# A two-layer graph network on one core: row-end products merged, identity products dropped, evictions moved

## The chip, the cores and the metric

The kernel runs on one core of a Trainium2 chip. The metric is the device time of one execution in microseconds (us). A core has five engines with queues of their own: PE (TensorE, matrix products), DVE (VectorE), ACT (ScalarE), POOL (GpSimd) and SP (SyncE, which here only issues DMAs). They meet through semaphores. Matrix products write to PSUM, eight banks of 512 f32 for each of 128 partitions; everything else lies in SBUF.

## The reference

`x` is 4096 nodes by 64 features, `adj` a 4096 by 4096 matrix of weights, under 1% of them not zero.

```python
h = relu(layernorm(x))
for k in range(2):                                  # layer 0, two hops
    h = tanh(concatenate([adj @ h, h], axis=1) @ W[k])
x = x + h
h = relu(layernorm(x))
support = h @ weight                                # layer 1
mask = adj != 0
rank = cumsum(mask, axis=1); deg = rank[:, -1:]
k = minimum(deg, 100); pos = rank - (deg - k)
w = mask * where(pos > 0, 0.5 ** (k - pos), 0.0)
out = x + w @ support + bias
```

So the dense matrix is used three times: twice with its values, and once as powers of two that depend on how many entries of the row come after.

## The kernel before, in words

Nodes are cut into 32 blocks of 128 (`NB`), four chunks of 8 blocks (`CB`, `NCH`). `adjA[I, n]` is the tile of row chunk I and block n, 128 by 1024 f32 (512 KB); a row chunk has 1024 output nodes, held in two halves of 512 columns (`C`, index c). PSUM holds accumulators `acc`/`accl` of three banks in a pool with two buffers (`pacc`), and two single banks, `one` and `two`.

**Sweep 1** (L370) takes the row chunks 0 to 3, each with 16 pairs of blocks, from the highest block to 0. For each pair: the DMA (1 MB, up to five pairs ahead, L396), the count of non-zero entries (`count_pair`, marks on DVE or ahead on ACT, kept as bytes in `codes`), and hop-0 products. Blocks whose hop-0 result isn't known yet multiply h alone into bank `acc[:, 2]` (`agg_pair`, L254, two 64-row products over 512 columns). Blocks of an earlier chunk (`fused`, L438) multiply `[h, x1]` (128 rows) into banks 0 and 1: hop 0 in the lower half of the partitions, hop 1's share in the upper.

When a row chunk ends, `finish_row` (L306) is queued; one step of it runs after each further pair. It copies S (bank 2) and F (banks 0, 1) out of PSUM, makes po = W0 products of S, F and of the node's own features in `pre1`, x1T = tanh(po); transposes x1T to nodes by a product with `ident` (`nodes`, L208); makes the hop-1 share po1 (features by nodes: `wz[:, 1, 1, 0]` with F, `wz[:, c, 1, 1]` with x1T) and keeps it in `pre1`; then `set_after` (L293) twice, with `tri` and with `neg`, from the totals of both halves and of the later half. Its output `after` is subtracted from the codes by `settle`. For the last row, `finish_last` (L473) does the same inside sweep 2; for row 0 the products of held blocks (`G`) are added.

**Sweep 2** (L771) computes hop 1 for the blocks not fused (72 blocks of 512 KB, ring of 6 then 4 slots) and, as soon as a chunk of x2 is ready, layer 1. `finish_x2` (L511) is a generator: identity products L518 bring the share in `pre1` into bank `py` as nodes, a second set L531 adds the rest, ACT takes tanh, DVE adds the residual `xres`, then a layer norm whose result is split in three bf16 parts: hi, mid (in `hx`) and lo. **Layer 1** goes in 64 units (J, g, n): chunk J of x2, row chunk g, two blocks. `convert` turns codes into powers of two, on DVE or ACT, into any free place (`spaces`). `layer1(n)` issues n units together: first all products of hi and mid (L692, `accl` banks 0 and 1, c = 0, 1), then all products of lo (L704, bank 2, c in the halves of the partitions). When the four units of a (J, g) are done and the sum isn't `kept` for the next J, its three banks are evicted into `part(g)`: a first one is copied by ACT and DVE (L725), later ones added by DVE (L729, L734). `finish_out` (L746) multiplies by `weight`, adds `pre1` and stores.

The order of the work is written by hand (`manual_schedule`): within sweep 1 by the pair loop, within sweep 2 by a planner that keeps a clock for each engine (`use`) and a list of due times (`chain`, `ready`, `due`), and emits conversions up to 2.5 to 10 us ahead of PE's clock (`lead`). Each engine runs what was emitted in that order; the waits between engines follow from the tiles.

Of the kernel before, what the change touches and what calls it, by code (L numbers as in the profile page):

```python
# [8 lines left out]
F32 = mybir.dt.float32  # L9
# [27 lines left out]
def gnn_kernel(  # L37
# [20 lines left out]

    nc = tc.nc

    N, D = x.shape
# [46 lines left out]
    xv = x.rearrange("(p b) d -> p b d", b=NB)  # L108
# [14 lines left out]
    def load_x(engine, b0, b1):  # L123
        engine.dma_start(pre1[:, b0:b1, :], xv[:, b0:b1, :])
# [7 lines left out]

    def load_weights():
        for h in range(2):
            rows = slice(h * D, (h + 1) * D)
            nc.sync.dma_start(wz[rows, h], Wd)
            nc.sync.dma_start(wa[rows], weight)
            nc.gpsimd.tensor_copy(wh[rows, h], wa[rows])

# [10 lines left out]
    ident = cpool.tile([P, P], F32, name="ident")  # L150
# [4 lines left out]
    neg = cpool.tile([P, P], BF16, name="neg")  # L155
    nc.vector.tensor_scalar(neg, diff, 0.0, -1.0, op0=ALU.is_equal, op1=ALU.mult)

    off = cpool.tile([P, 2], F32, name="off")
    for h in range(2):
        nc.vector.tensor_scalar(  # L160
            off[:, h : h + 1], diff[:, P - 1 : P], float(2 * FULL), float((1 - h) * FULL),
            op0=ALU.mult, op1=ALU.add,
        )
# [43 lines left out]

    def nodes(src):  # L208

        pt = one(name="pt")  # L210
        for t in range(TC):
            nc.tensor.matmul(  # L212
                pt[:, t * P : (t + 1) * P], by_t(src)[:, t // 2, t % 2, :], ident,
                start=True, stop=True, skip_group_check=True,
            )
        return pt.rearrange("p (t c e) -> p t c e", t=TC, c=NC)
# [67 lines left out]
    def totals(I):  # L284

        both = tmp([P, CW], U8, name="both")
        nc.vector.tensor_tensor(both.bitcast(U16), cnts[I % 2][0], cnts[I % 2][1], op=ALU.add)  # L287
        tot = [tmp([P, CW], BF16, name="tot") for _ in range(2)]
        nc.scalar.copy(tot[0], both)  # L289
        nc.scalar.copy(tot[1], cnts[I % 2][1].bitcast(U8))  # L290
        return tot

    def set_after(I, v, tot, banks):  # L293

        for c, pb in enumerate(banks):
            nc.tensor.matmul(  # L296
                pb, tri if v else neg, tot[1 - v][:, c * C : (c + 1) * C],
                start=v == 1, stop=True, skip_group_check=True,
            )
        for c, pb in enumerate(banks):  # L300
            nc.vector.tensor_scalar(  # L301
                after[:, v, I * CW + c * C : I * CW + (c + 1) * C], pb,
                off[:, v : v + 1], float(K), op0=ALU.add, op1=ALU.min,
            )

    def finish_row(I, acc, held):  # L306
        S = tmp(name="S")
        nc.scalar.copy(S, acc[:, NC, :])
        if I:
            F = [tmp(name="F") for _ in range(NC)]  # L310
            for c in range(NC):
                nc.scalar.copy(F[c], acc[:, c, :])
        tot = totals(I)
        yield
        po = one(name="po")
        terms = [(lambda c: wz[:, c, 0, 0], lambda c: S)]
        if I:
            terms.append((lambda c: wz[:, 0, 0, 0], lambda c: F[c]))
        x1T = x1_of(po, I, terms)
        po1 = two(name="po1")  # L320
        if I:
            for c in range(NC):
                nc.tensor.matmul(
                    po1[c * D : (c + 1) * D, :], wz[:, 1, 1, 0], F[c], start=True, stop=False
                )
        yield
        pt = nodes(x1T)
        for c in range(NC):
            nc.tensor.matmul(  # L329
                po1[c * D : (c + 1) * D, :], wz[:, c, 1, 1], x1T, start=I == 0, stop=I > 0  # L330
            )
        nc.scalar.copy(as_nodes(hx[:, chunk(I), D:]), pt)
        yield
        if I == 0:

            own = [v for k in sorted(held) for v in held[k]]
            for n, (b, a) in enumerate(own):
                agg_pair(acc[:, 0, :], hx[:, b, D:], a, n == 0, n == len(own) - 1)
            held.clear()
            G = tmp(name="G")  # L340
            nc.scalar.copy(G, acc[:, 0, :])
            yield
            for c in range(NC):
                nc.tensor.matmul(
                    po1[c * D : (c + 1) * D, :], wz[:, c, 1, 0], G, start=False, stop=True
                )
        nc.scalar.copy(flat(pre1[:, chunk(I), :]), po1)
        yield
        banks = [one(name="pb"), two(name="pb")]
        for v in (1, 0):  # L350
            set_after(I, v, tot, banks)
            yield
        all_settle(I)
# [16 lines left out]
    def sweep1():  # L370
        b0 = NB - 2
        load_x(nc.sync, b0, NB)
        load_x(nc.sync, NB - CB, b0)
# [26 lines left out]
        for k, (I, b) in enumerate(pairs):  # L400
# [3 lines left out]
            if k == 0:  # L404
                load(1, 0)
                load_x(nc.sync, NB - 2 * CB, NB - CB)
                load(2, 0)
                load_x(nc.sync, 0, NB - 2 * CB)
# [54 lines left out]
        return acc, totals(I)  # L463
# [9 lines left out]
    def finish_last(acc, tot):  # L473

        I = NCH - 1
        S = tmp(name="S")
# [4 lines left out]
        use("ACT", 1.7, 0.2)  # L481
# [7 lines left out]
        pt = nodes(x1T)  # L489
        nc.scalar.copy(as_nodes(hx[:, chunk(I), D:]), pt)  # L490
        use("ACT", 0.6, use("PE", 1.3) + 0.2)
        po1 = two(name="po1")
        for c in range(NC):
            nc.tensor.matmul(
                po1[c * D : (c + 1) * D, :], wz[:, 1, 1, 0], F[c], start=True, stop=False
            )
        for c in range(NC):
            nc.tensor.matmul(
                po1[c * D : (c + 1) * D, :], wz[:, c, 1, 1], x1T, start=False, stop=True
            )  # L500
        nc.scalar.copy(flat(pre1[:, chunk(I), :]), po1)
        use("ACT", 0.6, use("PE", 1.9) + 0.2)
        yield
        banks = [one(name="pb"), two(name="pb")]
        for v in (1, 0):
            set_after(I, v, tot, banks)
            use("DVE", 1.4, use("PE", 0.5) + 0.2)
            yield
        all_settle(I)

    def finish_x2(I, acc):  # L511

        h = chunk(I)

        pt = one(name="py")
        v = by_t(flat(pre1[:, h, :]))
        for t in range(TC):
            nc.tensor.matmul(  # L518
                pt[:, t * P : (t + 1) * P], v[:, t // 2, t % 2, :], ident,
                start=t == 0, stop=False, skip_group_check=True,  # L520
            )
# [3 lines left out]
        nc.sync.dma_start(xres, xv[:, h, :])  # L525
        t0 = use("ACT", 0.6, clock["PE"] + 0.2)
        use("PE", 1.25)
        yield t0 + 0.1
        v = by_t(S)
        for t in range(TC):  # L530
            nc.tensor.matmul(  # L531
                pt[:, t * P : (t + 1) * P].rearrange("p (c e) -> p c e", c=NC),
                v[:, t // 2, t % 2, :], wz[:, :, 1, 0, :],
                start=False, stop=True, skip_group_check=True,
            )
        y = tmp(name="y")
        nc.scalar.activation(y, pt, AF.Tanh)
        yield use("ACT", 0.65, use("PE", 1.25) + 0.2) - 0.5
        nc.vector.tensor_tensor(
            as_nodes(pre1[:, h, :]), as_nodes(xres), y.rearrange("p (t c e) -> p t c e", t=TC, c=NC),  # L540
            op=ALU.add,
        )
        t = use("DVE", 0.7, clock["ACT"] + 0.1)
# [132 lines left out]
    def layer1(n):  # L676
# [20 lines left out]
        use("PE", 0.2)  # L697
        for i, acc in zip(todo, accs):
# [10 lines left out]
        for i, acc in zip(todo, accs):  # L709
# [12 lines left out]
            if g not in parted:  # L722
                parted.add(g)
                for q, p in enumerate(part(g)):
                    (nc.vector.tensor_copy if q == 1 else nc.scalar.copy)(p, acc[:, q, :])  # L725
                    use("DVE" if q == 1 else "ACT", 0.65, t)
            elif J:
                for q, p in enumerate(part(g)):
                    nc.vector.tensor_tensor(p, acc[:, q, :], p, op=ALU.add)  # L729
                    use("DVE", 0.65, t)  # L730
            else:
                ys = part(g)
                for q, p in enumerate(ys):
                    nc.vector.tensor_tensor(p, acc[:, q, :], p, op=ALU.add)  # L734
                t = use("DVE", 1.9, t)
# [7 lines left out]

    outs = []

    def finish_out(g, ys):  # L746
        last = g == order[0][-1]
        pt = (one if g % 2 else two)(name="pto")
# [3 lines left out]
        for ks in [range(K4)] if not last else [range(K4 // 2), range(K4 // 2, K4)]:  # L752
            for k in ks:
                cols = slice(k * P, (k + 1) * P)
                for c in range(NC):
                    nc.tensor.matmul(  # L756
                        pt[:, k * P + c * D : k * P + (c + 1) * D], ys[c][:, cols], wa,
                        start=k == c == 0, stop=not last, skip_group_check=True,
# [12 lines left out]
    def sweep2(acc, tot):  # L771
# [7 lines left out]
        space(quad(mbuf.rearrange("p a r i -> p (a r i)").bitcast(I16)))  # L779
# [5 lines left out]
        last = finish_last(acc, tot)  # L785
# [92 lines left out]
    sweep2(*sweep1())  # L878
# [26 lines left out]
```

## Time and profile before

| what | us |
|---|---|
| median of 3 runs (lowest, highest) | 392.31 (390.9, 392.37) |
| profiled execution | 390.78 |
| its span | 389.0 |
| sweep 1 up to the last pair | 0 to 205.5 |
| layer 1 from its first product | 241.9 |
| last output stored | 387.95 |

In the profile, one f32 product is recorded as two matmuls, so `x8` under L254 is two blocks. Two 64-row products on different halves of the array run side by side: eight such records take 1.72 us, eight of 128 rows (L438) 3.48. Rates of the DMA queues from the page, in 40 slices of 9.7 us:

```profile
GB/s 229 415 411 406 365 408 407 409 408 409 410 345 270 313 327 235 205 291 305 293 350 317 250 417 401 182 283 305 304 265 224 313 312 258 2 2 2 0 56 54
```

The transfers are at their full rate, some 410 GB/s, up to about 110 us and again around 223 to 240.

### The profile page before, as it was taken

The numbers are of one execution on the slowest core, as the hardware profiler recorded it, in microseconds if no ns is written. First come the engines' busy times: TensorE is split into PE (matmuls) and PEld (weight loads), VectorE is DVE, ScalarE is ACT, GpSimd is POOL, SyncE is SP. The second block draws the span as 40 slices with busy tenths as digits, with TensorE's granted clock in tenths as the row PEclk, the third lists the DMA queues.
The fourth block names the chain that finished last, engine by engine and source line by source line (L and its number), as shares of the span: only waits on it lengthen the run. The fifth ranks groups of instructions, "written<-read, shape, count | busy, mean of one in ns | idle before, by whom it ended". The sixth has DMA issues, their size and how long they took to land.

```text
span 389.0 us, 4496 instructions
## 1 busy us (share of the span) xinstructions
PE 365.5 (94%) x1654; PEld 144.5 (37%) x1668; DVE 301.4 (77%) x565; ACT 166.2 (43%) x164; POOL 22.7 (6%) x21
## 2 busy tenths in 40 slices
PE   3698789999999999999999988999999999999995
PEld 0142223234333443444443323333343333434554
DVE  5979989499989999699889697777846844389943
ACT  2179980754363433410004111744246945388200
POOL 2202100000000000000000030300003000030000
PEclk9699999999999999999999999999999999999999
DMA  7999999999997896578999799588876887000011
GB/s 229 415 411 406 365 408 407 409 408 409 410 345 270 313 327 235 205 291 305 293 350 317 250 417 401 182 283 305 304 265 224 313 312 258 2 2 2 0 56 54
DMA packets 30150, 108.50 MB, mean 279 GB/s; under 512 B 2736, under 2 KB 3376, under 8 KB 30128
## 3 DMA queue, kind: packets, MB, share of 16 engines
q1 hardware_dynamic: 30128, 108.21, 75.0%
q8 instruction: 13, 0.21, 0.2%
q14 instruction: 9, 0.07, 0.1%
HBM read 107.15 MB, written 1.05 MB: 278 GB/s over the span
## 4 chain that ended last, share of the span: by engine, by line
PE 79%; DMA 13%; SPq 3%; ACT 2%; issue 1%; DVE 0%; ACTq 0%
PE acc L254 25%; PE acc L438 21%; PE accl L692 15%; PE accl L704 8%; DMA codes<-in_adjA_dram 8%; DMA ring<-in_adjA_dram 5%; SPq L396 3%; PE po L196 2%; PE pto L756 2%; PE pt L212 1%; ACT codes L227 1%; PE pb L296 1%; PE py L518 1%; ACT codes L228 1%; PE po L329 1%
## 5 line engine op out<-in xcount | busy, mean ns | idle before, releaser
L254 PE MATMUL acc<-ring,hx 128*64 128x512 f32 x384 | 95.6, 623 | 12.2 <-DVE hx L186 6.4
L438 PE MATMUL acc<-ring,hx 128*128 128x512 f32 x152 | 66.2, 593 | 0.0
L254 PE MATMUL acc<-codes,hx 128*64 128x512 f32 x256 | 59.3, 598 | 5.5 <-DMA codes<-in_adjA_dram 5.5
L254 PEld LDWEIGHTS acc<-ring,hx 128*64 128x64 f32 x384 | 25.6, 140 | 66.3 <-issue 31.6
L438 PEld LDWEIGHTS acc<-ring,hx 128*128 128x128 f32 x152 | 28.8, 190 | 36.0 <-issue 35.7
L248 DVE TENSOR_SCALAR lo<-codes 128x512 uint16<-128x512 uint16 x128 | 37.6, 294 | 4.4
L247 DVE TENSOR_TENSOR codes<-mbuf,lo 128x512 uint16<-128x512 uint16 x90 | 38.3, 425 | 3.1
L692 PEld LDWEIGHTS <-hx 128*128 128x128 bf16 x256 | 23.2, 98 | 39.7 <-issue 12.6
L366 DVE TENSOR_TENSOR codes<-codes,after 128x2048 uint16<-128x2048 uint16 x32 | 37.6, 1217 | 0.0
L183 POOL TENSOR_TENSOR s<-s,half 128x8 f32<-128x8 f32 (+2 forms) x9 | 16.7, 1852 | 323.1 <-DVE s L182 323.1
L236 DVE TENSOR_SCALAR mbuf<-ring 128x2048 uint8<-128x2048 f32 x27 | 32.9, 1220 | 2.0 <-DMA ring<-in_adjA_dram 2.0
L228 ACT ACTIVATE codes<-codes 128x1024 uint8<-128x1024 int8 x32 | 33.8, 1057 | 1.0
L254 PEld LDWEIGHTS acc<-codes,hx 128*64 128x64 f32 x256 | 17.7, 138 | 43.3 <-issue 30.5
L227 ACT ACTIVATE codes<-codes 128x1024 int8<-128x1024 f32 x24 | 25.1, 1047 | 16.1 <-DMA codes<-in_adjA_dram 16.1
L642 ACT ACTIVATE codes<-codes,zero 128x2048 int16<-128x2048 uint8 x14 | 27.2, 1992 | 9.7 <-PE accl L704 9.7
L692 PE MATMUL accl<-codes,hx 128*128 128x512 bf16 x118 | 29.2, 380 | 0.2
L642 ACT ACTIVATE ring<-codes,zero 128x2048 int16<-128x2048 uint8 x11 | 21.7, 1995 | 11.0 <-PE accl L704 11.0
L236 DVE TENSOR_SCALAR mbuf<-codes 128x2048 uint8<-128x2048 f32 x21 | 25.6, 1219 | 0.0
L301 DVE TENSOR_SCALAR after<-pb,off 128x512 uint8<-128x512 f32 x16 | 11.4, 745 | 13.3 <-PE pb L296 13.3
L289 ACT CAST tot<-both 128x1024 bf16<-128x1024 uint8 x4 | 4.2, 1057 | 37.7 <-DVE both L287 37.7
L692 PE MATMUL accl<-ring,hx 128*128 128x512 bf16 x74 | 18.8, 380 | 0.6 <-issue 0.2
L704 PEld LDWEIGHTS <-lo 128*64 128x64 bf16 x256 | 12.2, 109 | 19.0 <-issue 10.6
(109 smaller groups left out, 354.8 us busy)
## 6 DMA issues: line engine op xcount, KB each, us to landing
ring<-in_adjA_dram SPq DMA_DIRECT2D x74, 512.0 KB, 5.0
codes<-in_adjA_dram SPq DMA_DIRECT2D x33, 1024.0 KB, 12.5
ring<-in_adjA_dram SPq DMA_DIRECT2D x30, 1024.0 KB, 5.6
xres<-in_x_dram SPq DMA_DIRECT2D x4, 256.0 KB, 5.9
out_dram<-o SPq DMA_DIRECT2D x3, 256.0 KB, 2.5
pre<-in_x_dram SPq DMA_DIRECT2D x1, 512.0 KB, 9.8
pre<-in_x_dram SPq DMA_DIRECT2D x1, 256.0 KB, 6.8
out_dram<-o SPq DMA_DIRECT2D x2, 128.0 KB, 1.9
```

The source lines that it names most:

```text
L183: nc.gpsimd.tensor_tensor(s2, s2, half[:, :nb], op=ALU.pow)
L227: nc.scalar.activation(sign, a[:, r], AF.Sign)
L228: nc.scalar.activation(m, sign, AF.Square, scale=float((FLAG - 1 + 0.25) ** 0.5))
L236: nc.vector.tensor_scalar(m, a, 0.0, float(FLAG - 1), op0=ALU.not_equal, op1=ALU.mult)
L247: nc.vector.tensor_tensor(q, marks[r].bitcast(U16), cnt, op=ALU.add)
L248: nc.vector.tensor_scalar(cnt, q, 0x7F7F, None, op0=ALU.bitwise_and)
L254: nc.tensor.matmul(acc[c * D : (c + 1) * D, :], src, a[:, c * C : (c + 1) * C], start=first, stop=last,)
L366: nc.vector.tensor_tensor(q, q, a[:, None, :].to_broadcast([P, 4, CW // 2]), op=ALU.subtract)
L438: nc.tensor.matmul(acc[:, c, :], hx[:, g, :], a[:, r, c * C : (c + 1) * C], start=g == CB * I - 1, stop=g == 0,)
L642: nc.scalar.activation(w.rearrange("p r k x y -> p r k (x y)"), src.rearrange("p r (y k) -> p r k y", k=2), AF.Relu, scale=float(FLAG), bi ...
L692: nc.tensor.matmul(like(accs[-1][:, c, :], w), hm[:, CB * J + 2 * k + r, : 2 * D], w[:, r, c], start=first and r == 0, stop=last and r == 1,)
L704: nc.tensor.matmul(like(acc[c * D : (c + 1) * D, 2, :], w), lo[:, CB * J + 2 * k + r, :], w[:, r, c], start=first and r == 0, stop=last an ...
```

## The change

Six edits come together.

1. At the ends of rows 1 and 2 the sums are stacked: `T[c]` holds bank c's lower half over the c-th half of bank 2, so that one product with `w0` (hop 0's W twice) replaces two. The upper halves of banks 0 and 1 go to `Fx`.
2. `x1_and_share` multiplies x1T once with `both_w` = [ident, W1], 256 columns, into banks `one` and `two`: x1 as nodes and the share of hop 1, both by nodes. `take` copies each out in two parts. The share is kept by nodes in `pre1`, so `finish_x2` has no identity products; it adds the share on DVE before the tanh, and yields before its products, not after the first of them.
3. `set_after` uses `tri` only; the early half follows from the late one and the later half's count by three byte operations on DVE.
4. `x` is handed over as four chunks, [4, 128, 8, 64]; each is one DMA, and chunk 3 is loaded whole before the first tile.
5. In `layer1`, banks 0 and 1 of a finished sum are evicted between the hi and the lo products of the batch (`evict`), bank 2 after the lo products. First evictions are all on ACT.
6. The two halves of the last output use different banks.

```diff
-    def load_x(engine, b0, b1):
-        engine.dma_start(pre1[:, b0:b1, :], xv[:, b0:b1, :])
+    def load_x(q):
+        nc.sync.dma_start(pre1[:, chunk(q), :], x[q])
...
-    def set_after(I, v, tot, banks):
-
+    def set_after(I, tot, banks):
+
+        cols = slice(I * CW, (I + 1) * CW)
         for c, pb in enumerate(banks):
-            nc.tensor.matmul(
-                pb, tri if v else neg, tot[1 - v][:, c * C : (c + 1) * C],
-                start=v == 1, stop=True, skip_group_check=True,
-            )
+            nc.tensor.matmul(pb, tri, tot[:, c * C : (c + 1) * C], start=True, stop=True)
...
+        early = after[:, 0, cols]
+        nc.vector.tensor_scalar(
+            early.bitcast(U16), cnts[I % 2][1], -1.0, float(FULL * 257), op0=ALU.mult, op1=ALU.add
+        )
+        nc.vector.tensor_tensor(
+            early.bitcast(U16), early.bitcast(U16), after[:, 1, cols].bitcast(U16), op=ALU.add
+        )
+        nc.vector.tensor_scalar(early, early, float(K), None, op0=ALU.min)
+
+    def x1_and_share(I, x1T, Fx):
+
+        banks = [one(name="pt"), two(name="pt")]
+        v = by_t(x1T)
+        for h, pt in enumerate(banks):
+            pt = pt.rearrange("p (t w q) -> p t w q", t=2, w=2)
+            if Fx is not None:
+                f = by_t(Fx)
+                for t in range(2):
+                    nc.tensor.matmul(
+                        pt[:, t, 1, :].rearrange("p (c e) -> p c e", c=NC), f[:, h, t, :], wz[:, :, 1, 0, :],
+                        start=t == 0, stop=False, skip_group_check=True,
+                    )
+            for t in range(2):
+                nc.tensor.matmul(
+                    pt[:, t, :, :], v[:, h, t, :], both_w,
+                    start=Fx is None and t == 0, stop=True, skip_group_check=True,
+                )
+        return banks
...
+    def take(dst, banks, w):
+        for h, pt in halves_of(banks, w):
+            nc.scalar.copy(as_nodes(dst)[:, 2 * h : 2 * h + 2], pt)
+
     def finish_row(I, acc, held):
-        S = tmp(name="S")
-        nc.scalar.copy(S, acc[:, NC, :])
         if I:
-            F = [tmp(name="F") for _ in range(NC)]
+
+            T = [tmp(name="T") for _ in range(NC)]
             for c in range(NC):
-                nc.scalar.copy(F[c], acc[:, c, :])
-        tot = totals(I)
+                nc.scalar.copy(T[c][:D], acc[:D, c, :])
+                nc.scalar.copy(T[c][D:], acc[c * D : (c + 1) * D, NC, :])
+            Fx = tmp(name="Fx")
+            for c in range(NC):
+                nc.scalar.copy(Fx[c * D : (c + 1) * D], acc[D:, c, :])
+            terms = [(lambda c: w0, lambda c: T[c])]
...
     def finish_x2(I, acc):
 
         h = chunk(I)
-
-        pt = one(name="py")
-        v = by_t(flat(pre1[:, h, :]))
-        for t in range(TC):
-            nc.tensor.matmul(
-                pt[:, t * P : (t + 1) * P], v[:, t // 2, t % 2, :], ident,
-                start=t == 0, stop=False, skip_group_check=True,
-            )
         S = tmp(name="S")
         nc.scalar.copy(S, acc)
         xres = tmp([P, CB, D], name="xres")
-        nc.sync.dma_start(xres, xv[:, h, :])
-        t0 = use("ACT", 0.6, clock["PE"] + 0.2)
-        use("PE", 1.25)
-        yield t0 + 0.1
+        nc.sync.dma_start(xres, x[I])
+        yield use("ACT", 0.6, clock["PE"] + 0.2) + 0.1
+
+        pt = one(name="py")
...
-        y = tmp(name="y")
-        nc.scalar.activation(y, pt, AF.Tanh)
-        yield use("ACT", 0.65, use("PE", 1.25) + 0.2) - 0.5
+        y = tmp([P, CB, D], name="y")
         nc.vector.tensor_tensor(
-            as_nodes(pre1[:, h, :]), as_nodes(xres), y.rearrange("p (t c e) -> p t c e", t=TC, c=NC),
+            as_nodes(y), pt.rearrange("p (t c e) -> p t c e", t=TC, c=NC), as_nodes(pre1[:, h, :]),
             op=ALU.add,
         )
+        nc.scalar.activation(y, y, AF.Tanh)
+        t = use("DVE", 0.7, use("PE", 1.15) + 0.2)
+        yield use("ACT", 0.65, t + 0.1) - 0.5
+        nc.vector.tensor_add(pre1[:, h, :], xres, y)
...
             use("PE", 0.9, max(made[i][1], ready[J]))
         use("PE", 0.2)
+
+        for i, acc in zip(todo, accs):
+            J, g, k = units[i]
+            if k == CB // 2 - 1 and (J, g) not in kept:
+                evict(J, g, acc, (0, 1))
         for i, acc in zip(todo, accs):
             J, g, k = units[i]
             first, last = k == 0 and (J + 1, g) not in kept, k == CB // 2 - 1 and (J, g) not in kept
...
             del sums[g]
-            if g not in parted:
-                parted.add(g)
-                for q, p in enumerate(part(g)):
-                    (nc.vector.tensor_copy if q == 1 else nc.scalar.copy)(p, acc[:, q, :])
-                    use("DVE" if q == 1 else "ACT", 0.65, t)
...
+            t = evict(J, g, acc, (2,))
+            if J == 0:
                 ys = part(g)
...
+    def evict(J, g, acc, qs):
+        t = clock["PE"] + 0.2
+        new = g not in parted
+        for q in qs:
+            p = part(g)[q]
+            if new:
+                nc.scalar.copy(p, acc[:, q, :])
+                t = use("ACT", 0.65, t)
+            else:
+                nc.vector.tensor_tensor(p, acc[:, q, :], p, op=ALU.add)
+                t = use("DVE", 0.65, t)
+        if 2 in qs:
+            parted.add(g)
+        return t
...
         for ks in [range(K4)] if not last else [range(K4 // 2), range(K4 // 2, K4)]:
+            pt = (one if (g + bool(ks.start)) % 2 else two)(name="pto")
```

## The prediction, made before the changed kernel was run

> **What bounds the kernel now.** I read the page first, then the chain of waits in order of time, then the PE groups by line, then the landing of each DMA beside the matmul that uses it.
>
> ```profile
> PE 365.5 (94%) x1654; PEld 144.5 (37%) x1668; DVE 301.4 (77%) x565; ACT 166.2 (43%) x164; POOL 22.7 (6%) x21
> PE 79%; DMA 13%; SPq 3%; ACT 2%; issue 1%; DVE 0%; ACTq 0%
> ```
>
> Busy PE says little alone; the chain says that PE's own work sets 79% of the span. In order of time it leaves PE in two places only: up to 54.9 us (landing of the first row of adjacency) and at the head of sweep 2:
>
> ```profile
> 222.94 1.21 PE L518 MATMUL py<-ident,pre 128*128 128x128 f32 x8
> 225.02 1.97 PE L254 MATMUL acc<-ring,hx 128*64 128x512 f32 x8
> 227.19 1.08 PE L254 MATMUL acc<-ring,hx 128*64 128x512 f32 x4 [0.20 <-DMA ring<-in_adjA_dram]
> ...
> 238.71 1.08 PE L254 MATMUL acc<-ring,hx 128*64 128x512 f32 x4 [0.20 <-DMA ring<-in_adjA_dram]
> 239.72 1.21 PE L518 MATMUL py<-ident,pre 128*128 128x128 f32 x8
> ```
>
> From 227 to 239 us blocks start 1.28 us apart, at the rate of landing; PE time saved inside that stretch is lost. Elsewhere (54.9 to 223, 240 to 386) a microsecond of PE is a microsecond of span, in both directions. In row 1 the tiles land 3.6 us or more ahead of their matmul once the held products are done, so about 1 us of PE saved at the first row end still passes.
>
> The products that the change touches:
>
> ```profile
> L518 PE MATMUL py<-ident,pre 128*128 128x128 f32 x32 | 4.8, 294 | 0.0
> L212 PE MATMUL pt<-ident,x1T 128*128 128x128 f32 x32 | 4.8, 294 | 0.0
> L296 PE MATMUL pb<-tot,neg 128*128 128x512 bf16 x8 | 2.4, 383 | 0.0
> ```
>
> And one eviction of a finished layer-1 sum:
>
> ```profile
> 337.08 1.05 PE L704 MATMUL accl<-codes,lo 128*64 128x512 bf16 x8
> 338.07 1.90 PE L692 MATMUL accl<-codes,hx 128*128 128x512 bf16 x8
> 338.18 1.89 DVE L729 TENSOR_TENSOR codes<-accl,codes 128x512 f32<-128x512 f32 x3 [5.50 <-PE accl L704]
> ```
>
> PE ends its lo products and goes straight to the hi products of the next sum, in the other accl buffer; the 1.89 us eviction lies beside them and costs PE nothing. And from the waits:
>
> ```profile
> DVE codes L725 <- ACT codes L725: 7.2, 4, 2.5
> ```
>
> Two engines copy different banks of one accl tile, and each waits for the other: waits are placed by tile, not by bank.
>
> [...] the copy of S waits at 54.87 us behind a marking activation although its sum was finished. [...]
>
> **The change part by part**, in the profiled execution (390.78 us: span 389.0 and 1.78 around it; the median of the runs shown is 392.31).
>
> Unit prices from the chain: a 64-row f32 pair over 512 columns 0.86; four 128-column f32 products 0.94 to 1.14. Four 256-column ones aren't in the trace: estimated from half of a 512-column pair's price each, 4 x 0.43 = 1.72 (bounds 1.7 and 2.0).
>
> *Row ends 1 and 2.* Before: po 2.58, hop-1 share 0.86 + 1.01, transposes 1.14 = 5.59. After: po in two pairs 1.72, Fx products 0.94, merged 1.72 = 4.38. New in front of po: four half-height copies on ACT instead of one whole S. No 64-row ACT copy is in the trace; the 64-row DVE add L740 (686 ns) costs what the 128-row one does (683), so I take 0.56 each, 2.3 us in all against 1.72 of cover (the next pair's products): PE stalls 0.6 (0 to 1.1). The neg product, 0.54, goes. Sum: 4.98 - 5.59 - 0.54 = -1.1 each, -2.2. The four quarter copies out of the merged banks (about 1.5 us, estimated from 0.58 for 512 elements) lie beside the next pair.
>
> *Row end 0.* Merged 1.72 for 2.15, G product 0.94 for 0.86, neg 0.54 gone; pb now waits for two copies behind four marking activations, as it did for one (0.68): -0.8.
>
> *Row end 3.* 2.66 for 3.01, neg 0.54 gone: -0.9. It frees ring slots earlier and so passes through the DMA stretch.
>
> *x2 (four times).* The identity product L518, 1.14, goes. The one at 223 us saves nothing, DMA is late next. Its py also comes a pair later, behind the G blocks, with one more DVE add (0.68) on its chain: high and mid parts of h2 are ready some 1.3 us later than before and a settle may hold the chain; the first layer-1 unit, 24 blocks in, then waits about 0.4. The other three pass: -3.4. S's copy has no cover of its own any more, but the program order puts a pair or two units between.
>
> *x by chunks.* Same bytes, same number of DMAs. The first LN now waits for 256 KB rather than 64 KB: its 2 blocks were ready at 6.33 us, I take 1.5 to 2 later; the landing of pairs 2 to 16 hides it (PE waits for DMA until 53 us): 0, up to +0.5.
>
> *DVE in set_after.* Two 745 ns reads become three cheaper operations of 0.3 to 0.6: 0.
>
> *Tail.* The last output's second half gets its own bank: the 0.52 wait at 383.9 goes, -0.5.
>
> *Evictions.* They move between the hi and the lo products of the same batch. In the instruction order of the changed program the first lo product of each such batch waits for the second of the two evictions (its semaphore value is that eviction's), and behind it stand all of PE's instructions. There are 12 evicted sums (16 less 4 kept): 4 first ones, now wholly on ACT, 8 on DVE. Price of one: hand-over 0.05, two operations, hand-over 0.05. DVE 2 x 0.61 + 0.07 of tail = 1.29, so 1.35; ACT 1.1, so 1.2. Sum 8 x 1.35 + 4 x 1.2 = 15.6 us. Nothing covers it: what used to cover the eviction was the next sum's hi products, now behind the wait.
>
> To that comes what stands in the evicting queue. From the order on each engine I follow two: the first eviction sits on ACT behind x2's tanh, a 2 us conversion into mbuf, the LN square and another 2 us conversion, all chained to py: about 3.3 more. The second of J=1 on DVE sits behind the three LN operations of the last x2: 1.25 more. In the trace of before, 9 of 12 evicting engines were already idle when the hi products ended; of the other three one is the first, and in the changed order two conversions instead of five, and one addition behind its own output, stand before the other two. I add no more.
>
> Sum: -0.8 - 2.2 - 0.9 + 0.4 - 3.4 - 0.5 = -7.4; +15.6 + 4.6 = +20.2. Net +12.8: 390.8 becomes **403.5 us**.
>
> **Rivals.** (a) *The wait costs nothing*: the change then gives its -7.4, 383.4 us. For it: [...] evictions were wholly hidden. Against: the semaphore and PE's program order. Break-even is 7.4 / 12 = 0.62 us a sum, less than one DVE eviction of the two; the opposite sign needs the stall to be under half of my price, say because the wait is met early. Chance 0.07.
>
> (b) *Stalls without queueing, row ends at their best*: no T stall (-1.2), no extra 4.6: 397.7. Chance 0.25.
>
> (c) *Evictions stand behind conversions*: decode runs up to 5 to 10 us ahead of PE, one conversion is 1.5 us on DVE and 2 on ACT. If four more are met half-way and one in full, +5: 408.5. Before, 3 of 12 had over 1 us in front (1.3, 3.5 and 1.3). Chance 0.2.
>
> (d) *Both cancel*: stalls of some 0.6, within 0.5% of before. Chance 0.03.
>
> **How the numbers follow.** The likeliest, 403.5 (own range 400 to 406.5), has 0.45. For 8 in 10 the range takes in (b) and most of (c): 397 to 409. About 0.5% (2 us) is what a measurement of this kernel tells from no change. Faster 0.07 from (a), same 0.03 from (d), slower 0.90.
>
> **What would show it.** In the changed trace: a PE gap of 1.2 to 1.4 us before the lo products, 12 times, released by the eviction; over 4 us at the first. Row ends without neg and with four 256-column records in 1.72 us; a gap of about 0.6 before po in rows 1 and 2, released by ACT; no identity product at x2; the last landing of I=2 in sweep 2 some 3.5 to 4 us earlier than 238.67. It is wrong if PE passes the lo products without a gap, if the row-end copies stop PE by over 1 us, or if x2's longer chain leaves PE waiting for h2.

## The result, and the profile after

After the change the kernel takes 409.3 us (median of 4 runs, 408.7 to 410.77) against 392.34 us before: ratio 1.0444, 95% interval 1.0405 to 1.0483, so 17.0 us slower. The profiled execution has a span of 407.5 us against 389.0. The forecast was 403.5 with a range of 397 to 409: the sign is right, and so is the mechanism of the stalls; the size is 5.8 us short, just outside the range.

The page of the changed kernel, its line of busy time and its line of TensorE's clock in 40 slices:

```profile
PE 362.3 (89%) x1606; PEld 147.6 (36%) x1620; DVE 302.5 (74%) x573; ACT 167.7 (41%) x176; POOL 24.6 (6%) x24
...
PEclk9999999999999999999999998999999999989999
```

TensorE is busy for 3 us less than before (365.5) in a span that is 18.5 us longer, so nearly all of what was added is waiting. And two slices far from the start, at about 250 and 356 us, have a lower granted clock; before, there was nothing of the kind between the first 20 us and the end of the work.

The waits of PE in the changed kernel (what waits, for what: us in total, times, longest):

```profile
PE accl L715 <- DVE codes L753: 11.9, 8, 2.3
PE accl L715 <- ACT codes L750: 6.9, 4, 3.4
```

L715 are the lo products, L750 and L753 the evictions of banks 0 and 1. It is 12 stalls, 18.8 us. Ten of them are 1.16 (ACT) or 1.38 us (DVE); one is 3.39, one 2.28. The longest in the timeline (start, duration, engine and line; in brackets the idle time before and what ended it):

```profile
244.47 1.02 PE L698 MATMUL accl<-mbuf,hx 128*128 128x512 bf16 x4 [0.46 <-ACT mbuf L648]
...
245.35 0.63 ACT L180 ACTIVATE sq<-xc 128x512 f32<-128x512 f32 x1 [0.93 <-DVE xc L179]
245.88 1.99 ACT L648 ACTIVATE ring<-codes,zero 128x2048 int16<-128x2048 uint8 x1
...
247.77 1.05 ACT L750 COPY codes<-accl 128x512 f32<-128x512 f32 x2
248.88 0.62 PE L715 MATMUL accl<-hx,lo 128*64 128x512 bf16 x4 [3.39 <-ACT codes L750]
249.31 0.62 PE L715 MATMUL accl<-mbuf,lo 128*64 128x512 bf16 x4
...
249.74 5.32 PE L245 MATMUL acc<-ring,hx 128*64 128x512 f32 x16
```

The hi products end at 245.5. ACT is then in a square, takes a 2.0 us conversion behind it, and makes both copies after that; only then do the lo products start, which write a third bank that neither copy touches. The last line is the second surprise: 16 records, two pairs of blocks, take 5.32 us, where they stand at 3.4 to 3.7 elsewhere. The same stretch by windows (us, PE's busy time, then the other engines; the number in the middle is the granted clock):

```profile
246.50:249.90 3.40, 1.02 (x10) 0.74 (x11) 0.61 (x3) 2.33 (x3) 0.00 (x0) 1.00 0.02 8
249.90:253.30 3.40, 3.40 (x12) 1.18 (x9) 3.27 (x9) 0.59 (x1) 0.00 (x0) 0.50 0.24 49
...
352.30:355.70 3.40, 1.34 (x10) 0.62 (x10) 2.22 (x5) 2.56 (x3) 0.00 (x0) 1.00 0.00 0
355.70:359.20 3.50, 3.50 (x12) 1.12 (x11) 3.40 (x9) 3.50 (x2) 0.72 (x1) 0.51 0.02 5
```

Behind each of the two long stalls TensorE runs at half its clock (0.50 granted) for 3.41 us and loses 1.7 us of work, 3.4 in all; the expectations below call such a stretch a half-clock window.

Where the two executions stand, by the time at which PE reaches a point:

| PE reaches | before | after |
|---|---|---|
| products of row end 0 | 55.49 | 54.24 |
| row end 1 | 104.02 | 102.03 |
| row end 2 | 152.53 | 149.81 |
| row end 3 | 207.30 | 204.51 |
| end of the 24th block of sweep 2 | 239.72 | 236.46 |
| next pair of blocks behind the first two units | 244.41 | 241.00 |
| last product | 385.53 | 404.04 |

Up to 241 us the change gains 3.4 us; from there on it loses 22.

### The profile page after: what moved, and what is told of

The parts are those of the page before. It is cut to its first block, busy times and chain, and to the rows that moved or that the text cites. A ratio compares the mean times of both kernels' runs of the same rounds, so it can differ in the third digit from the quotient of the medians.

```text
span 407.5 us, 4423 instructions
## 1 busy us (share of the span) xinstructions
PE 362.3 (89%) x1606; PEld 147.6 (36%) x1620; DVE 302.5 (74%) x573; ACT 167.7 (41%) x176; POOL 24.6 (6%) x24
## 3 DMA queue, kind: packets, MB, share of 16 engines
HBM read 107.15 MB, written 1.05 MB: 266 GB/s over the span
## 4 chain that ended last, share of the span: by engine, by line
issue 47%; PE 33%; DVE 9%; DMA 4%; ACT 2%; POOL 2%; SPq 0%; POOLq 0%; DVEq 0%; ACTq 0%
PE accl L698 13%; PE acc L245 10%; PE accl L715 8%; DMA wa<-in_weight_dram 4%; DVE codes L753 3%; PE pto L771 2%; POOL s L184 2%; ACT ring L648 1%; ACT codes L750 1%; DVE mbuf L227 1%; PE py L535 1%; DVE s L178 1%; DVE codes L238 1%; DVE xc L179 1%; DMA pre<-in_x_dram 1%
## 5 line engine op out<-in xcount | busy, mean ns | idle before, releaser
L245 PE MATMUL acc<-codes,hx 128*64 128x512 f32 x256 | 60.3, 598 | 8.2 <-DMA codes<-in_adjA_dram 6.5
L245 PEld LDWEIGHTS acc<-ring,hx 128*64 128x64 f32 x384 | 27.4, 141 | 65.2 <-issue 33.8
L753 DVE TENSOR_TENSOR codes<-accl,codes 128x512 f32<-128x512 f32 x24 | 15.8, 687 | 30.1 <-PE accl L698 17.5
L648 ACT ACTIVATE codes<-codes,zero 128x2048 int16<-128x2048 uint8 x13 | 25.3, 1990 | 8.5 <-PE accl L715 8.5
L648 ACT ACTIVATE ring<-codes,zero 128x2048 int16<-128x2048 uint8 x10 | 20.0, 1995 | 20.5 <-PE accl L715 14.9
L715 PEld LDWEIGHTS <-lo 128*64 128x64 bf16 x256 | 14.5, 110 | 37.2 <-issue 30.5
L715 PE MATMUL accl<-codes,lo 128*64 128x512 bf16 x124 | 16.8, 383 | 9.2 <-DVE codes L753 9.2
L698 PE MATMUL accl<-ring,hx 128*128 128x512 bf16 x77 | 20.6, 401 | 0.3
```

The source lines that it names most:

```text
L245: nc.tensor.matmul(acc[c * D : (c + 1) * D, :], src, a[:, c * C : (c + 1) * C], start=first, stop=last,)
L648: nc.scalar.activation(w.rearrange("p r k x y -> p r k (x y)"), src.rearrange("p r (y k) -> p r k y", k=2), AF.Relu, scale=float(FLAG), bi ...
L698: nc.tensor.matmul(like(accs[-1][:, c, :], w), hm[:, CB * J + 2 * k + r, : 2 * D], w[:, r, c], start=first and r == 0, stop=last and r == 1,)
L715: nc.tensor.matmul(like(acc[c * D : (c + 1) * D, 2, :], w), lo[:, CB * J + 2 * k + r, :], w[:, r, c], start=first and r == 0, stop=last an ...
```

## The experiments

My theory after the comparison: the wait of the lo products on the evictions of the same batch is the whole loss, with the two stretches of half clock behind it. The rival: the row ends, x2 and the layout cost more than they save. All twelve runs are told here; ratios are to the kernel before.

**Evictions back behind the lo products.** Everything else of the change stays.

```diff
-            if k == CB // 2 - 1 and (J, g) not in kept:
-                evict(J, g, acc, (0, 1))
...
-            t = evict(J, g, acc, (2,))
+            t = evict(J, g, acc, (0, 1, 2))
```

> The changed kernel with one thing undone: the evictions of all three banks come behind the lo products again. Theory (the lo products' wait is the loss): the 12 stalls of 18.8 us in all go, with them the two half-clock windows (3.4 us) and the restarts (0.8), so 409.3 - 23.0 = about 386, some 6 us below the kernel before, and TensorE's clock stays full between 25 us and the end. Rival (the row ends, x2 or the layout cost more than they save, and the gaps only move idle time that was there anyway): it stays near 400 to 409. If the half clock has another cause than the stalls, it stays: 389 to 390.

Measured: 387.65 us, ratio 0.9881 (0.9849 to 0.9914). The timeline of this run at the same place:

```profile
244.53 1.02 PE L698 MATMUL accl<-mbuf,hx 128*128 128x512 bf16 x4 [0.46 <-ACT mbuf L648]
...
245.48 0.62 PE L711 MATMUL accl<-hx,lo 128*64 128x512 bf16 x4
...
246.37 1.88 PE L245 MATMUL acc<-ring,hx 128*64 128x512 f32 x8
```

No gap ahead of the lo products, and the pair of blocks behind them takes 1.88 us; TensorE's clock stays full from 9.4 us to the end of the work (mean granted clock 0.998 of the whole run, 0.991 in the changed kernel). The same kernel, measured once more:

> The changed kernel with the evictions behind the lo products, once more beside the run with the old cut of the loads: 387.0 to 388.3, ratio 0.986 to 0.990. If it came to 390 or more, the difference to the run with x loaded as before would be one of the occasion and not of the layout.

Measured: 389.81, ratio 0.9922 (0.9903 to 0.9942), so my narrow expectation missed: two measurements of one kernel, each against the kernel before beside it, lay 0.4% (1.6 us) apart. The eviction edit thus costs 1.0444 less 0.9922 or 0.9881, 20.5 to 22.1 us, and the rest of the change gains 3.1 to 4.7 us, not the 7.4 of my sum.

**The kernel before with the eviction edit alone** (edit 5 whole: the first evictions are all on ACT here too).

```diff
+            if k == CB // 2 - 1 and (J, g) not in kept:
+                evict(J, g, acc, (0, 1))
...
+            t = evict(J, g, acc, (2,))
```

> The kernel before with one part of the change alone: the first two banks are evicted ahead of the lo products of the same batch. Theory: its lo products wait for the second eviction 12 times as well, at 1.16 to 1.38 us each plus what stands in the evicting queue, 15.6 to 19 us[...]: 392.3 + 16 to 23 = 408 to 415. Rival (evictions cost nothing by themselves, the loss is from row ends and x2): 392.

Measured: 410.07, ratio 1.0464 (1.0425 to 1.0502), +18.2 us. Its waits:

```profile
PE accl L708 <- DVE codes L746: 11.9, 8, 2.1
...
PE accl L708 <- ACT codes L743: 5.7, 4, 2.2
```

17.6 us in the same 12 stalls. The edit alone reproduces the loss; the rival is out. The 16 to 23 us of that expectation left room for half-clock stretches of 1.7 us each on top of the stalls. None follows here amid the work (mean granted clock 0.998): its two longest stalls are 2.24 and 2.09 us. In the changed kernel one followed a stall of 2.28; the last section comes back to it.

**Each accumulator as two PSUM tiles.** Banks 0 and 1 in one, the lo bank in another; the evictions stay ahead of the lo products.

```diff
-                acc = pacc.tile([P, 3, C], F32, tag="acc", name="acc")
+                acc = Acc("acc")
...
+            if q < 2:
+                    self.ab = pacc.tile([P, 2, C], F32, tag="acc", name=self.name)
...
+                self.lo = pacc.tile([P, C], F32, tag="acc_lo", name=self.name)
```

> The changed kernel with every accumulator as two PSUM tiles, one with banks 0 and 1, one with the lo bank; the evictions stay ahead of the lo products. Theory (the wait comes from one tile holding all three banks, not from the hardware): lo products start without a gap, 384 to 387 us, as with the evictions behind the lo products or a little less. Rival (the chip itself holds PE while another engine reads a neighbouring bank): gaps of over 1 us before lo products stay, 400 or more.

Measured: 387.33, ratio 0.9876 (0.9844 to 0.9908). The timeline at one of the last sums:

```profile
364.71 3.62 PE L712 MATMUL accl<-codes,hx 128*128 128x512 bf16 x16
...
368.26 1.92 PE L729 MATMUL accl<-codes,lo 128*64 128x512 bf16 x16
368.37 1.29 DVE L767 TENSOR_TENSOR codes<-accl,codes 128x512 f32<-128x512 f32 x2 [2.53 <-PE accl L712]
```

The two evictions start 0.11 us after the lo products and lie wholly beside them: what the edit was meant to be. This is shown, not argued: here the chip doesn't hold PE while DVE reads neighbouring banks (1.29 us of DVE beside 1.92 us of lo products, with no gap ahead of them); the wait of 18.8 us was the program's, by tile. But 387.33 against 387.65 with the evictions behind: with nothing to wait for, the earlier eviction brings nothing that can be measured, since an eviction behind the lo products was hidden too.

**Only the two longest stalls taken away.** The sums (3,0) and (1,3) are evicted behind their lo products, the other ten ahead.

```diff
-            if k == CB // 2 - 1 and (J, g) not in kept:
+            if k == CB // 2 - 1 and (J, g) not in kept and (J, g) not in [(3, 0), (1, 3)]:
```

> The changed kernel with only the two longest stalls taken away: the evictions of the sums (3,0) and (1,3) come behind their lo products, the other ten stay ahead. Theory A [...]: no half-clock window is left, -3.39 - 2.28 - 3.4 - 0.1 = -9.2, 400.1 us. Theory B (the halved clock comes from elsewhere, such as the sum of several stalls): the windows stay at about 250 and 356 us or move, -5.8, 403.5 us.

Measured: 401.84, ratio 1.0256 (1.0216 to 1.0296), between the two. Its waits:

```profile
PE accl L715 <- DVE codes L753: 9.7, 7, 1.4
PE accl L715 <- ACT codes L750: 4.2, 3, 1.8
```

For the clock it is as Theory A had it: no half-clock stretch is left amid the work (mean granted clock 0.998). The stalls fell only from 18.8 to 13.9, because the next sum on ACT now waits 1.83 us instead of 1.16, and a wait of 0.74 us for h2 came up at 360 us. Sum: -4.9 - 3.4 + 0.7 = -7.6; the span fell by 7.0.

**The changed kernel once more,** with no edit:

> The changed kernel once more, for a second profile. Theory [...]: the 12 stalls are there again within 0.1 us each, while the half-clock windows may number 0, 1 or 2[...]; the span is 404 to 407.5. Rival [...]: two windows again, behind the same two stalls.

Measured: span 405.2 us, one run of 407.02. The 12 stalls are there again, each within 0.1 us, but only one half-clock stretch, behind the 3.39. The stall of 2.28 us at 351.43 is followed by full clock. The run by windows:

```profile
350.00:353.40 3.40, 1.43 (x7) 0.57 (x6) 3.33 (x6) 1.08 (x3) 0.00 (x0) 1.00 0.01 2
353.40:356.80 3.40, 3.08 (x20) 1.28 (x21) 2.22 (x5) 3.40 (x2) 0.00 (x0) 1.00 0.02 5
```

So it isn't the length of the stall alone: the rival falls. That the count might differ between two executions was my estimate, and it did: two stretches in the first, one in this. What decides isn't shown.

**The layout of x alone** (edit 4 whole, with the order of the loads), on the kernel before:

```diff
-        engine.dma_start(pre1[:, b0:b1, :], xv[:, b0:b1, :])
+        nc.sync.dma_start(pre1[:, chunk(q), :], x[q])
```

> The kernel before with x laid out by chunks alone. Theory from the trace of the changed kernel, where pair 16 of row 0 came 1.2 us earlier: the first slice of the span moves more bytes and the landings of row 0 move forward, 1.2 us less (0.8 to 1.7), ratio 0.996 to 0.998. Rival (my forecast's step): no change, up to 0.5 us slower.

Measured: 390.17, ratio 0.994 (0.9916 to 0.9963), -2.3 us: a gain, rather larger than the theory's 1.2. Row end 0 is reached at 54.33 instead of 55.49. Then the converse, the changed kernel with late evictions and x loaded as before:

```diff
-        load_x(NCH - 1)
+        load_x(nc.sync, b0, NB)
+        load_x(nc.sync, NB - CB, b0)
...
-        nc.sync.dma_start(xres, x[I])
+        nc.sync.dma_start(xres, xv[:, h, :])
```

> The changed kernel with the evictions behind the lo products and with x loaded as before: what is left of the change is the row ends, the shares kept by nodes, x2 and the tail. Theory (these give only about 2 us, since two thirds of their saving comes back as waits for S, for h2, for the copies and for DMA): 389.5 to 390.5, ratio 0.993 to 0.997. Rival (they give the 7.4 us that my sum had for them, and the layout of x nothing): 385. Rival two (they give nothing, all of the gain is the layout of x): 392.3.

Measured: 392.45, ratio 1.0005 (0.999 to 1.002), against 0.9881 and 0.9922 with the new layout: rival two. With x loaded as before, row ends, shares by nodes, x2 and tail together bring nothing. The parts don't quite add up: 2.3 us and nothing, where the change without its evictions gains 3.1 to 4.7; what is missing is about as much as two measurements of one kernel differ by. The trace of this run shows something else: PE waits 2.68 us for a block at 221.65, and a half-clock stretch follows, again of 3.41 us.

```profile
222.36:225.77 3.41, 1.34 (x6) 0.42 (x8) 0.01 (x1) 0.00 (x0) 0.00 (x0) 1.00 1.03 420
225.77:229.18 3.41, 3.41 (x12) 1.78 (x8) 0.00 (x0) 0.00 (x0) 0.00 (x0) 0.50 1.03 419
```

So half clock (0.50) followed a wait for a DMA here as it followed the evictions. PE waits for a landing again at 235.5, so that this stretch by itself cost time isn't shown.

Between these two stands a run with the layout of the change but the loads at the start cut and ordered as before:

```diff
-        load_x(NCH - 1)
+        nc.sync.dma_start(pre1[:, b0:, :], x[NCH - 1][:, CB - 2 :, :])
+        nc.sync.dma_start(pre1[:, NB - CB : b0, :], x[NCH - 1][:, : CB - 2, :])
```

> The changed kernel with the evictions behind the lo products and x by chunks, but with the loads of x at the start cut and ordered as in the kernel before (2 blocks, 6 blocks, one chunk, two chunks at once). Theory A (of what the layout of x gives in the changed kernel, the part at the start comes from the cut of the loads, the other part from the slice that x2 reads while DMA is the limit, which lands 0.7 us behind its forerunner instead of 2.3 to 2.9): pair 16 of row 0 back by about 1.2 us to 53 or later, the slice at 0.7 to 1.8 us; 388.9 against 387.7. Theory B (all of it from the start): 391.5 to 392.5. Theory C (all from the layout of the slice): 387.5.

Measured: 389.87, ratio 0.9924 (0.9907 to 0.9942). In its trace both halves of theory A are there: row end 0 is at 55.64 as with the old cut, and the first slice for x2 lands 0.65 us behind its forerunner. Over all traces, row end 0 is reached at 55.5 to 56.3 us with the old cut of the loads (4 kernels) and at 53.7 to 54.6 with the new one (10 profiles); the first slice of x for x2, in a stretch where the blocks land every 1.28 us and DMA sets the pace, lands 2.26 to 2.94 us behind the block before it from the old layout (3 kernels) and 0.65 to 0.73 from the new (9 of 11 profiles; the other two 1.48 and 1.76). The three later slices take 0.6 to 1.1 in both. But the run's time is that of the kernel with the new cut measured beside it (389.81), as theory C had it, so the 1.2 us at the start didn't reach the end there.

**Own features first in the row ends,** on top of the two PSUM tiles:

```diff
-        paired(po, terms + [(lambda c: wz[:, c, 0, 1], lambda c: flat(pre1[:, chunk(I), :]))])
+        paired(po, [(lambda c: wz[:, c, 0, 1], lambda c: flat(pre1[:, chunk(I), :]))] + terms)
```

> The changed kernel with each accumulator as two PSUM tiles, and in the row ends the products of the own features ahead of those of the copied sums. Theory: in rows 1 and 2 the pairs of po no longer wait behind the four half-height copies, which stand 2.3 us on ACT against 1.9 us of cover; each of the two row ends is 0.7 to 0.9 us shorter, row 0 up to 0.2: 385.5 to 386.0 against 387.3. Rival (the products' own price, not the copies, is what the row ends kept): no change within 0.3.

Measured: 386.34, ratio 0.9866 (0.9826 to 0.9905). The row end of row 1 in the changed kernel:

```profile
100.96 0.58 ACT L333 COPY T<-acc 64x512 f32<-64x512 f32 x1
101.56 0.58 ACT L332 COPY T<-acc 64x512 f32<-64x512 f32 x1
102.03 1.40 PE L197 MATMUL po<-T,w 128*64 128x512 f32 x3
102.15 0.58 ACT L333 COPY T<-acc 64x512 f32<-64x512 f32 x1
...
103.27 0.59 PE L197 MATMUL po<-T,w 128*64 128x512 f32 x1
```

and with own features first:

```profile
101.98 1.03 PE L211 MATMUL po<-pre,wz 128*64 128x512 f32 x4
102.10 0.58 ACT L347 COPY T<-acc 64x512 f32<-64x512 f32 x1
...
102.84 1.03 PE L211 MATMUL po<-T,w 128*64 128x512 f32 x4
```

The last copy ends at 102.73; the product that reads it used to stand ahead of the others and now follows them. From row end 1 to row end 2 PE needs 47.10 us instead of 47.78, from 2 to 3 54.00 instead of 54.70: 0.7 us each, as expected; row end 0 gained nothing. In the medians this is within the spread.

**The stacking undone,** again on the two tiles: rows 1 and 2 take the three whole sums.

```diff
-            terms = [(lambda c: w0, lambda c: T[c])]
+            terms = [(lambda c: wz[:, c, 0, 0], lambda c: S), (lambda c: wz[:, 0, 0, 0], lambda c: F[c])]
```

> As the run with two PSUM tiles, but the first products of rows 1 and 2 take the three whole sums again instead of the stacked half-height ones: one more pair of products (+0.86 each) against one ACT copy less (-0.58) and no wait for it. Theory (the stacking gave nothing, since its copies cost what its products save): within 0.5 us of 387.3. Rival (the stacking saves its 0.86 a row): 389.0.

Measured: 388.43, ratio 0.9911 (0.9882 to 0.994). By the medians it lies between theory and rival, and can't decide. By the trace, row end to row end takes 47.83 and 54.95 us against 47.78 and 54.71 with the stacking: 0.05 and 0.24 longer, where the extra pair of products alone is 0.86. The stacked sums, as ordered in the change, gave next to nothing.

**Cover for the copy of S,** on the two tiles with own features first: one pair of layer-1 units where the identity product used to stand.

```diff
                 chain.append((next(gen), gen))
+                if I == 1:
+                    layer1(2)
```

The changed kernel has these two waits, which the kernel before doesn't have:

```profile
PE acc L245 <- ACT S L527: 0.9, 1, 0.9
PE accl L698 <- DVE hx L566: 0.6, 1, 0.6
```

> As the run with two PSUM tiles and own features first, with one layer-1 unit pair issued right behind the last sum of row 1 in sweep 2, where the removed identity product used to stand. Theory (the identity product hid the copy of S, which stands behind a 2.0 us conversion on ACT, and its removal laid the wait open): the 0.9 us wait of PE for S near 284 us goes, 385.4 against 386.3 in the same units, ratio near 0.984. Rival (PE waits there for something else that comes as late, such as a DMA): the wait shows under another name and the time stays.

Measured: 386.14, ratio 0.9849 (0.9819 to 0.9879). The timeline there:

```profile
283.21 1.04 PE L712 MATMUL accl<-ring,hx 128*128 128x512 bf16 x4
283.57 0.57 ACT L541 COPY S<-acc 128x512 f32<-128x512 f32 x1
...
286.03 1.21 PE L549 MATMUL py<-wz,S 128*128 128x128 f32 x8
```

PE goes on with units while ACT copies; the wait is gone, and nothing took its place. From the pair of blocks ahead of it until three pairs, the two units and py are done, PE takes 9.35 us (281.40 to 290.75), against 10.23 (281.95 to 292.18) without the cover. This is the fastest of all kernels here, 1.5% under the kernel before; the three versions with two tiles (0.9876, 0.9866, 0.9849) can't be told apart by their intervals.

## Why the forecast was right in kind and short in size

In the profiled execution the forecast's sum was +12.8 and the change measured +18.5. By the medians it is +17.0; of the 5.8 us that the forecast is short there, 1.6 are its base, the profiled execution of 390.78 us, which lies below the median of 392.34. By its steps:

*Evictions, 15.6 + 4.6 = +20.2.* Right: 12 stalls, none left out, 18.8 us. DVE 1.38 for my 1.35, ACT 1.16 for 1.2. Nothing covered them, as forecast: while the first lo product waits from 245.49 to 248.88 us, PE is busy for 0.00 us. First queueing: 3.39 in all, where I had 1.2 + 3.3: when the hi products ended, only a square and one conversion were left in front, not the whole chain. Second: 2.28 for my 2.6. Rivals (a) and (d) are out by the stalls themselves; of (c), nothing: no other eviction met a conversion.

*What the sum left out: the clock, +3.4.* This is the first of the two steps that failed. I priced a stall as its own length; the prediction doesn't name the clock, and so puts this term at nothing without a reason. The trace has it: two stretches of 3.41 us at 0.50 of the clock, behind stalls of 3.39 and 2.28 us. The records show some 0.07 us more at each restart, an estimated 0.8 in all: without a stall the lo products start that much ahead of the recorded end of the hi products (with two tiles at 368.26, against 364.71 + 3.62), and at each of the 12 stalls this overlap is lost.

*"= -7.4" for the other parts.* This is the other failed step: -4.5 in that profile (+18.5 less 18.8 of stalls, 3.4 of clock and 0.8 of restarts), -3.1 to -4.7 in the medians.

- Row end 0: -0.8 forecast, -0.74 measured (row end to row end, 48.53 to 47.79).
- Row ends 1 and 2: -1.1 each forecast, -0.73 and -0.07 measured. My 0.6 for the wait behind the four copies was right (0.7, by the run with own features first), and so was the price of a half-height copy (0.58 for 0.56). Too low was the price of the new products, 2.66: with Fx they took 2.88 (the merged ones 1.84 for 1.72, those of Fx 1.04 for 0.94). In row 2 the products that go had been priced too high as well (neg 0.54 where the trace before has 0.43, the share with x1T 1.01 for 0.91), and the accumulation around the new ones lost some 0.4 more, which I can't place.
- Row end 3, -0.9, and "passes through the DMA stretch": from its start to the 24th block -0.47, and even that isn't its own. With x as before the same step came to +1.1 (206.61 to 240.1, against 207.30 to 239.72): PE waits the 2.68 us for a block at 221.65 there. The saving met a transfer that was late anyway.
- x2, "The other three pass: -3.4", and "the program order puts a pair or two units between" for the copy of S: this failed. The product went at each of them, 1.0 us, but it had been a cover. Waits of 0.60 for h2 (forecast 0.4) and 0.91 for S came up, and 0.7 to 1.2 for the last h2 in those kernels in which the stalls didn't hide it. The run with cover for S shows the middle one.
- x by chunks, "0, up to +0.5": wrong in sign. It gains 2.3 us by itself; in the trace 1.25 at the start and up to 2 at the first slice for x2.
- Tail, -0.5: as forecast, the wait for the output's first half is gone.

With x as before the edits other than the evictions add up to nothing (1.0005), so row ends and x2 were worth about 0 to 2 us and not 7.4; the layout, priced at nothing, brought most of what the change gained. These two errors partly cancel. What stays open: why the first slice of x lands so late from the old layout while the later ones don't, which of the loads at the start makes the 1.2 us, and why that gain doesn't reach the end in one pair of runs. No run here tells.

## What to carry to other kernels

Work that read one part of a tile and work that wrote another were held apart here by the tile (12 stalls, 18.8 us; none with two tiles); before an eviction is moved up beside products into its own accumulator, give the two parts tiles of their own, or leave it where the next sum hides it. A product that is removed may have been the cover of a copy: look up what stood beside it, and behind which queue that copy now waits. And price a stall on TensorE with the clock behind it: as an estimate from these numbers, two stalls of 1.4 us cost 2.8, and one of 2.8 may cost 4.5, with the 1.7 us that a half-clock stretch lost.

## What the runs showed of the hardware

*Half clock behind a stall.* Each of the three half-clock stretches listed below lasts 3.41 us in the clock's records, at 0.50, and begins 1.05 to 1.44 us after PE is back at work. Stalls of PE between 60 us and the end of the work, and the clock behind them (us):

| kernel | stall of PE | clock behind |
|---|---|---|
| changed | 3.39, to 248.88 | half from 249.93 |
| evictions late, x as before | 2.68, to 224.33 | half from 225.77 |
| changed | 2.28, to 354.36 | half from 355.74 |
| changed, again | 2.28, to 353.71 | full |
| evictions alone | 2.24 | full |
| two stalls late | 1.83 | full |

The ten stalls of 1.16 and 1.38 us in the changed kernel were followed by full clock too. A stall of 2.28 us was followed by half clock once and by full clock once, in the same program, so its length isn't all that decides; what else does isn't shown.

*Half the rows, the same time.* ACT's copies of 64 rows out of PSUM took as long here as those of 128:

```profile
L332 ACT COPY T<-acc 64x512 f32<-64x512 f32 x4 | 2.3, 580 | 16.9 <-PE acc L456 16.8
```

against 0.57 to 0.62 us for 128 rows of 512 elements in the same trace (0.565 to 0.587 for S, 0.605 to 0.620 for the own features); half the columns (128 rows of 256) took 0.37 to 0.38 us in the mean.
